# Graph attention on one core: logits of sources added and weights turned on TensorE, one exponential a batch, one more tile by columns

## The chip, the core and the metric

The kernel runs on one core of a Trainium2 chip. The core has engines that run side by side and wait for each other through semaphores: TensorE (PE in the profile; its weight loads are PEld), VectorE (DVE), ScalarE (ACT), GpSimd (POOL) and SyncE (SP). The metric is the device time of one execution in microseconds, lower is better; the time of a kernel is the median of several runs.

## The reference

A graph of 12,500 nodes has 412,500 edges, sorted by their target. Each node has 128 features in four heads of 32, each edge 64.

```python
h = jnp.maximum(_layernorm(x, axis=-1), 0.0)
h = (h @ W_node.T).reshape(num_nodes, H, HD)            # H = 4, HD = 32
e = (edge_features @ W_edge.T).reshape(num_edges, H, HD)
att = jnp.sum(jnp.concatenate([h[src], h[tgt], e], -1) * a, axis=-1)
att = jnp.where(att > 0, att, 0.2 * att)
m = jnp.maximum(segment_max(att, tgt), 0.0)
ex = jnp.exp(att - m[tgt])
denom = segment_sum(ex, tgt) + (num_edges - deg)[:, None] * jnp.exp(-m)
out = x + segment_sum((ex / denom[tgt])[:, :, None] * h[src], tgt)
```

An edge's logit is a sum of three parts: one of its source, one of its target, one of the edge itself. The weights of a target's edges are normed over the edges of that target, and the sources' rows are added up with these weights.

## The kernel before, in words

**Ahead of the loop** the kernel makes a table in device memory with a row of 144 numbers for each node: for each head the 32 projected features, two columns of ones and the two parts of the logit. The normed node features, turned (feature by node), also stay in SBUF as `features`.

**Batches.** The edges are cut into 461 chunks of 896 edges (7 tiles of 128), and 7 chunks make a batch, so 66 batches of 49 tiles. The loop over batches is written out. The order of the instructions on each engine is the order of the calls in that loop (lines 1328 to 1407); no scheduler moves them, and the engines meet only where one waits for a semaphore.

**Rows.** A tile of a batch needs the table rows of its 128 sources in the row buffer `hs`. There are three row buffers, so the rows of batch b + 3 can be brought when the scatter of batch b is done. Rows come in three ways. Most tiles are gathered by POOL (`gather`, one indirect DMA for a tile, line 334); ahead of them stands a memset of one column (`gate`, line 819) that waits for that scatter. One tile of a batch (three quarters of it in even batches) is brought row by row by SP, 32 single-row DMAs at a time (`row_by_row`, line 864), in turn with the loads of the edge features `eft` (line 760). The rest is made anew: ACT (line 885) and DVE (line 883) copy the sources' columns out of `features` one by one into `turned`, at addresses that they read into registers in groups of 32 (TENSOR_LOAD, line 852), and PE multiplies `turned` with the projection `wall` (`put_back`, line 904), whose result ACT copies into `hs` (line 905). `TURNED` says how many tiles come this way: 4 in odd batches, 3 and a quarter in even ones.

**Who copies columns when.** `OF_SCALAR` gives the groups of 32 copies that ACT does in an even and an odd batch, `OF_VECTOR` those of DVE. ACT's stand in `of_scalar` calls between its other work, and what is left is done at the end of the batch (line 1392), so ahead of the next batch's exponential. DVE's stand at named places, of which the first so many in `BEHIND` are taken.

**One batch** runs so. `begin` has PE multiply the edge features (lines 935 and 938), two batches ahead; `choose` has PE add the targets' logits (line 795), one batch ahead. `weigh` and `weigh_part` (lines 962 to 1026) make the weights: DVE copies the sources' logits out of `hs`, turns them (a transpose of blocks of 32), adds them to the product in four parts, applies the leak, finds each target's maximum by two scans (forward and back) and subtracts it (line 1014); ACT takes the exponential in four parts (line 1016); DVE forms the maxima at each target's end in four parts (line 1018) and turns both (line 1021). `mark` makes the one-hot matrix `hot` of the targets (line 958). `collect` has ACT copy the sums of the batch before out of PSUM (line 1120). `scatter` has DVE multiply the rows with the weights, two tiles and then five (line 1089), and PE add them up through `hot` (line 1095), after `collect` has emptied the same PSUM columns. Every second batch `merge` adds two batches' sums to what their targets have so far.

Of the kernel before, what the change touches and what calls it, by code (L numbers as in the profile page):

```python
# [9 lines left out]
F32 = mybir.dt.float32  # L10
# [4 lines left out]
OP = mybir.AluOpType  # L15
# [62 lines left out]
TURNED = 4  # L78
OF_SCALAR = (10, 9)
OF_VECTOR = (5, 5)  # L80
BEHIND = ("rows", "first", "near", "hot", "down", "up")
# [78 lines left out]
def kernel(  # L160
# [567 lines left out]
    both_ps = bank[:, :2 * T * R].rearrange("p (w t r) -> p w t r", w=2, t=T)  # L728
    ex_ps = both_ps[:, 0, :, :]
# [253 lines left out]
    def open_weights(s):  # L983

        s.zst = work.tile([P, T, R], F32, name="zst")
        a = work.tile([P, BUF], F32, name="a")
        s.att, s.m = a[:R, :CE], a[R:2 * R, :CE]
        s.up = ps.tile([P, BANKS * 512], F32, name="up")[:R, :CE]
        s.both = work.tile([P, 2, T, R], F32, name="both")

    def weigh_part(s, t0, t1):

        zst, att, up, m, both = s.zst, s.att, s.up, s.m, s.both
# [3 lines left out]
        def grouped(what, g):  # L997
            return what.rearrange("r (t g i) -> r g t i", g=NQT, i=R)[:, g, t0:t1, :]
# [8 lines left out]
        nc.vector.tensor_scalar(att[:, e0:e1], up[:, e0:e1], 0.2, None, op0=OP.mult)  # L1007
        on_half(s, nc.vector.tensor_tensor(z, up[:, e0:e1], att[:, e0:e1], op=OP.max))  # L1008
# [6 lines left out]
        for g in range(NQT):  # L1015
            nc.scalar.activation(both[g * R:(g + 1) * R, 0, t0:t1, :], grouped(att, g), AF.Exp)  # L1016
        for g in range(NQT):
            nc.vector.scalar_tensor_tensor(both[g * R:(g + 1) * R, 1, t0:t1, :], grouped(s.pen[:, 1:], g), -1.0 / BIG,  # L1018
                                           grouped(up, g), op0=OP.mult, op1=OP.mult)
        if t1 - t0 == T:  # L1020
            nc.vector.transpose(both_ps.rearrange("p w t r -> p (w t r)"), both.rearrange("p w t r -> p (w t r)"))  # L1021
        else:
            for w in range(2):
                nc.vector.transpose(both_ps[:, w, t0:t1, :].rearrange("p t r -> p (t r)"),  # L1024
                                    both[:, w, t0:t1, :].rearrange("p t r -> p (t r)"))
        nc.vector.tensor_copy(own, both_ps[:, 1, t0:t1, :s.chunks * H].rearrange("p t (q h) -> p t q h", h=H))
# [56 lines left out]
    def scatter(s):  # L1083
# [3 lines left out]
        for t0, t1 in ((0, FIRST), (FIRST, T)):  # L1087
# [3 lines left out]
            of_vector("rows" if t1 == T else "first")  # L1091
# [215 lines left out]
    with tc.manual_schedule():  # L1307
# [20 lines left out]
        for b in range(NBT - 1):  # L1328
# [30 lines left out]
            if b < NBT - 2:  # L1359
                mark(s)  # L1360
# [29 lines left out]
            if b == NBT - 3:  # L1390
                mark(batch(b + 1))
            of_scalar(spare[ENG.Activation])
# [309 lines left out]
```

## Time and profile before

| | |
|---|---|
| time, median of 3 runs | 6768.51 us (6765.73 to 6787.56) |
| the profiled execution: its own time, its span | 6719.83 us, 6718.1 us |
| busy, share of the span: PE, DVE, ACT, POOL | 27%, 40%, 38%, 42% |
| copies of single columns: ACT (L885), DVE (L883) | 18624 of 187 ns, 9888 of 142 ns |
| gathers by POOL (L334, from the table) | 2887 of 947 ns |
| row-by-row DMAs by SP (L864) | 7072 |
| scatter on PE (L1095) | 1820 of 680 ns |

The busy time is an average over stages that differ, and no engine is busy for half of the span. What matters in a kernel like this is the chain of waits from batch to batch: who waits for whom at the points where buffers are handed over. A row of the timeline gives the start, the time from the first start to the last end, the engine, the line, the operation, the tile written and read with its shape, the count, and in brackets how long the engine was idle before and what ended that. "issue" means that the profile shows nothing that the engine waited for.

### The profile page before, as it was taken

What the parts mean: (1) busy time and instruction counts of PE and PEld (TensorE: products, weight loads), DVE (VectorE), ACT (ScalarE), POOL (GpSimd) and SP (SyncE); (2) the same over time, 40 slices, a digit from 0 to 9 for tenths busy, and PEclk for the clock granted to TensorE, in tenths of its full rate; (3) what the DMA queues carried; (4) which work ended last, traced back from release to release, by engine and by line L of the source; (5) the groups of instructions that cost most, each with busy time, mean ns of one, the idle gap of its engine ahead of it and who ended that gap; (6) DMA issues with size and microseconds to landing.
All of it is one profiled execution on the core that took longest, in us unless ns stands there. A gap on an engine that the chain in (4) does not pass through costs nothing. (4 is left out here: it accounts for less than half of the span.)

```text
span 6718.1 us, 65140 instructions
## 1 busy us (share of the span) xinstructions
PE 1803.4 (27%) x4569; PEld 724.3 (11%) x4569; DVE 2718.8 (40%) x13514; ACT 2583.9 (38%) x20492; POOL 2797.8 (42%) x3018
## 2 busy tenths in 40 slices
PE   4223123223123232222232232133123223312323
PEld 3101001011011011010011011011011001101111
DVE  4434334344344243353343344344334334434445
ACT  4134334334344344344344344344334434433420
POOL 4453443343443443533533443443453353344351
PEclk8566566566566566665666566566566566656666
DMA  4322222222222222222222222222222222222221
GB/s 115 94 61 58 61 61 64 61 61 62 57 63 65 59 64 60 64 65 57 64 66 61 65 66 61 62 63 61 67 64 65 59 61 67 62 66 65 64 66 43
DMA packets 225620, 432.22 MB, mean 64 GB/s; under 512 B 92316, under 2 KB 125094, under 8 KB 225144
## 3 DMA queue, kind: packets, MB, share of 16 engines
q0 software_dynamic: 94240, 216.84, 13.5%
q1 hardware_dynamic: 100664, 145.09, 7.4%
q10 hardware_dynamic: 30240, 66.08, 2.8%
q14 instruction: 438, 3.59, 0.2%
q8 instruction: 38, 0.62, 0.0%
HBM read 412.21 MB, written 15.53 MB: 64 GB/s over the span
## 5 line engine op out<-in xcount | busy, mean ns | idle before, releaser
L885 ACT COPY turned<-features 128x1 f32 x18624 | 2053.1, 187 | 3473.0 <-issue 3469.9
L334 POOL DMA_INDIRECT hs<-table,ends x2887 | 2734.6, 947 | 1006.8 <-issue 895.0
L819 POOL MEMSET gate<- 128x1 f32 x63 | 6.2, 99 | 2758.7 <-PE pa L1095 2751.6
L1095 PE MATMUL pa<-hs,hot 128*128 128x504 f32 x1820 | 937.0, 680 | 531.5 <-ACT r L1120 478.6
L904 PE MATMUL more<-wall,turned 128*128 128x144 f32 x430 | 155.5, 457 | 3011.5 <-ACT hs L905 2985.0
L883 DVE COPY turned<-features 128x1 f32 x9888 | 681.8, 142 | 691.9 <-issue 689.8
L1021 DVE STREAM_TRANSPOSE exr<-both 128x448 f32<-128x448 f32 x65 | 42.9, 660 | 1530.4 <-ACT both L1016 1529.8
L1095 PEld LDWEIGHTS pa<-hs,hot 128*128 128x128 f32 x1820 | 398.5, 223 | 1045.4 <-issue 505.2
L1089 DVE TENSOR_TENSOR hs<-hs,exr 128x1848 f32<-128x1848 f32 (+1 forms) x130 | 456.6, 3515 | 0.0
L904 PEld LDWEIGHTS more<-wall,turned 128*128 128x128 f32 x430 | 91.5, 265 | 3093.8 <-ACT hs L905 3027.1
L938 PE MATMUL z<-eft,wa 128*32 128x512 f32 (+1 forms) x792 | 354.4, 592 | 61.5 <-DMA eft<-in_ef 61.4
L935 PE MATMUL z<-eft,wa 128*64 128x512 f32 (+1 forms) x132 | 85.6, 738 | 960.1 <-DMA eft<-in_ef 814.5
L1014 DVE TENSOR_TENSOR a<-z,a 32x896 f32<-32x896 f32 (+1 forms) x67 | 71.7, 1070 | 643.5 <-issue 643.3
L1120 ACT COPY r<-pa 32x70 f32<-32x70 f32 (+1 forms) x1040 | 263.6, 253 | 119.3 <-PE pa L1095 88.2
L1004 DVE TENSOR_TENSOR up<-z,zst 32x224 f32<-32x224 f32 (+2 forms) x268 | 104.3, 389 | 429.8 <-PE z L795 418.9
L795 PE MATMUL z<-near_dst,near_rows 128*32 128x512 f32 (+1 forms) x528 | 214.7, 550 | 30.5 <-DVE run L1154 22.6
L1018 DVE SCALAR_TENSOR_TENSOR both<-pen_sb,up 32x224 f32<-32x224 f32 (+2 forms) x268 | 100.3, 374 | 202.2 <-issue 201.7
L1016 ACT ACTIVATE both<-a 32x224 f32<-32x224 f32 (+2 forms) x268 | 102.8, 384 | 172.1 <-DVE a L1014 126.1
L789 DVE TENSOR_TENSOR near_dst<-near_dst,least 128x1792 f32<-128x1792 int32 x66 | 132.4, 2006 | 20.3 <-DMA near_dst<-in_dstc 20.3
L958 DVE TENSOR_TENSOR hot<-exr,key 128x1568 f32<-128x1568 f32 x65 | 116.4, 1791 | 59.3 <-PE pa L1095 57.1
L1009 DVE TENSOR_TENSOR_SCAN up<-pen_sb,z 32x896 f32<-32x896 f32 (+1 forms) x67 | 133.6, 1994 | 2.3
L1194 DVE TENSOR_TENSOR acc<-acc,up 128x70 f32 x461 | 105.1, 228 | 70.7 <-issue 48.6
(203 smaller groups left out, 1503.4 us busy)
## 6 DMA issues: line engine op xcount, KB each, us to landing
hs<-table SPq DMA_DIRECT2D x7072, 0.6 KB
eft<-in_ef SPq DMA_DIRECT2D x231, 448.0 KB
near_dst<-in_dstc ACTq DMA_DIRECT2D x128, 448.0 KB
hs<-table,ends POOLq DMA_INDIRECT x2887
near_rows<-near SPq DMA_DIRECT2D x461, 0.5 KB
pen_sb<-pens SPq DMA_DIRECT2D x66, 98.1 KB
xg<-in_xh SPq DMA_DIRECT2D x13, 448.0 KB
out<-xg SPq DMA_DIRECT2D x13, 448.0 KB
```

Source lines behind the costliest of these rows:

```text
L334: load = nc.gpsimd.indirect_dma_start(out=rows, out_offset=None, in_=of[:, :], in_offset=bass.IndirectOffsetOnAxis(ap=at, axis=0), engine_ ...
L789: nc.vector.tensor_tensor(hot, s.near_dst.bitcast(I32), least[:, s.b, :, None].to_broadcast([P, 2, CE]), op=OP.is_equal)
L795: s.made = own_half(s, nc.tensor.matmul(s.z[:, part], near_rows[:, s.b % 2, k, :], hot[:, k, part], start=False, stop=(k == 1), skip_group ...
L883: nc.vector.tensor_copy(s.turned[:, i:i + 1], column)
L885: nc.scalar.copy(s.turned[:, i:i + 1], column)
L904: nc.tensor.matmul(back_ps, s.turned[:, i * P:(i + 1) * P], wall, start=True, stop=True)
L938: s.made = own_half(s, nc.tensor.matmul(s.z[:, part], wa3[:, j + s.b % 2 * (SB + 1), :], s.eft[:, j, part], start=False, stop=(j == NEXT - ...
L958: nc.vector.tensor_tensor(s.hot.rearrange("p t q r -> p (t q) r"), rows_ps[:, None, :].to_broadcast([P, T * CB, W]), key[:, :, None].to_br ...
L1009: on_half(s, nc.vector.tensor_tensor_scan(up[:, e0:e1], s.pen[:, e0:e1], z, 0.0, op0=OP.add, op1=OP.max))
L1089: nc.vector.tensor_tensor(rows, rows, ex_ps[:, t0:t1, :CB * H, None].to_broadcast([P, t1 - t0, CB * H, HB]), op=OP.mult)
L1095: scattered[s.b] = nc.tensor.matmul(wide_ps[:, g, :], s.hot[:, t, g * NEXT:g * NEXT + SB, :].rearrange("p q r -> p (q r)"), flat[:, at:at ...
L1120: nc.scalar.copy(r[h * W:(h + 1) * W, q:q + NEXT * len(of) - NEXT + 1:NEXT, :], block)
```

## The change

`TURNED` becomes 5: odd batches make five tiles by columns, even ones four and a quarter, and POOL gathers one tile less in each batch (45 and 44 become 44 and 43). `OF_SCALAR` becomes (10, 10) and `OF_VECTOR` (9, 8): in an even and in an odd batch ACT does 10 and 10 groups of copies, not 10 and 9, and DVE 9 and 8, not 5 and 5. `BEHIND` has new places on DVE: "middle" (between the products of the scatter), "own" (after the sources' logits are copied), "up" (after the first scan), and, in even batches, "leaky" (ahead of it); "end" is named but not reached.

The sources' logits are no longer turned and added by DVE: PE multiplies them with the identity and adds the result to the product in PSUM (new line 998). ACT takes one exponential over 32 partitions and 896 columns (new line 1011), DVE forms the maxima in one step (1012), into the lower half of the same tile `both`, and PE turns both together in seven transposes (1015). `mark` moves into `weigh_part`, behind these transposes in the program's text. The products of the scatter are made for two, two and three tiles.

```diff
-TURNED = 4
-OF_SCALAR = (10, 9)
-OF_VECTOR = (5, 5)
-BEHIND = ("rows", "first", "near", "hot", "down", "up")
+TURNED = 5
+OF_SCALAR = (10, 10)
+OF_VECTOR = (9, 8)
+BEHIND = ("rows", "first", "near", "middle", "hot", "own", "down", "up", "leaky", "end")
...
-    both_ps = bank[:, :2 * T * R].rearrange("p (w t r) -> p w t r", w=2, t=T)
-    ex_ps = both_ps[:, 0, :, :]
+    both_ps = bank[:, :2 * T * R].rearrange("p (t w r) -> p t w r", w=2, t=T)
+    ex_ps = both_ps[:, :, 0, :]
...
-        s.both = work.tile([P, 2, T, R], F32, name="both")
+        s.both = work.tile([2 * R, CE], F32, name="both")
...
-        nc.vector.transpose(zst[:, t0:t1, :].rearrange("p t i -> p (t i)"),
-                            logits[:, t0:t1, :].rearrange("p t i -> p (t i)"))
-        for g in range(NQT):
-            on_half(s, nc.vector.tensor_tensor(grouped(up, g), grouped(s.z, g),
-                                               zst[g * R:(g + 1) * R, t0:t1, :], op=OP.add))
+        for t in range(t0, t1):
+            s.made = own_half(s, nc.tensor.matmul(s.z[:, t * P:(t + 1) * P], logits[:, t, :], ident,
+                                                  start=False, stop=True, skip_group_check=True))
+        of_vector("own")
         z = s.z[:, e0:e1]
-        nc.vector.tensor_scalar(att[:, e0:e1], up[:, e0:e1], 0.2, None, op0=OP.mult)
-        on_half(s, nc.vector.tensor_tensor(z, up[:, e0:e1], att[:, e0:e1], op=OP.max))
+        on_half(s, nc.vector.tensor_scalar(att[:, e0:e1], z, 0.2, None, op0=OP.mult))
+        on_half(s, nc.vector.tensor_tensor(z, z, att[:, e0:e1], op=OP.max))
+        of_vector("leaky")
...
-        for g in range(NQT):
-            nc.scalar.activation(both[g * R:(g + 1) * R, 0, t0:t1, :], grouped(att, g), AF.Exp)
-        for g in range(NQT):
-            nc.vector.scalar_tensor_tensor(both[g * R:(g + 1) * R, 1, t0:t1, :], grouped(s.pen[:, 1:], g), -1.0 / BIG,
-                                           grouped(up, g), op0=OP.mult, op1=OP.mult)
-        if t1 - t0 == T:
-            nc.vector.transpose(both_ps.rearrange("p w t r -> p (w t r)"), both.rearrange("p w t r -> p (w t r)"))
...
+        nc.scalar.activation(both[:R, e0:e1], att[:, e0:e1], AF.Exp)
+        nc.vector.scalar_tensor_tensor(both[R:, e0:e1], s.pen[:, e0 + 1:e1 + 1], -1.0 / BIG, up[:, e0:e1],
+                                       op0=OP.mult, op1=OP.mult)
+        for t in range(t0, t1):
+            nc.tensor.transpose(both_ps[:, t, :, :].rearrange("p w r -> p (w r)"), both[:, t * P:(t + 1) * P],
+                                ident[:2 * R, :2 * R])
+        if s.b < NBT - 2:
+            mark(s)
...
-        for t0, t1 in ((0, FIRST), (FIRST, T)):
+        for t0, t1 in ((0, FIRST), (FIRST, 2 * FIRST), (2 * FIRST, T)):
...
-            of_vector("rows" if t1 == T else "first")
+            of_vector("rows" if t1 == T else "middle" if t0 else "first")
...
-            if b < NBT - 2:
-                mark(s)
...
                 put_back(later, 3)
+                put_back(later, 4)
...
+            of_vector("end")
```

How the change stands on the engines is shown for an even batch. On PE, from the edge product of a later batch (L938) to the next addition of targets (L795), before:

```order
L938 MATMUL z<-eft,wa_84 32x384 x3
L904 MATMUL more<-wall,turned 128x144 x3
L909 MATMUL more<-wall,turned 32x144
L1095 MATMUL pa<-hs,hot 128x504 x14
L795 MATMUL z<-near_dst,near_rows 32x512 x2
```

and now:

```order
L938 MATMUL z<-eft,wa_84 32x384 x3
L998 MATMUL z<-ident,logits 32x128 x7
L1015 MATMUL exr<-ident,both 128x64 x7
L904 MATMUL more<-wall,turned 128x144 x4
L909 MATMUL more<-wall,turned 32x144
L1088 MATMUL pa<-hs,hot 128x504 x14
L795 MATMUL z<-near_dst,near_rows 32x512 x2
```

The addition of the sources' logits (L998) now stands behind the edge product, and the first product of the columns (L904) behind the transposes of the weights (L1015).

On ACT, from the last copies ahead of the exponential, before:

```order
L885 COPY turned<-features 128x1 x32
L1016 ACTIVATE both<-a 32x224 x4
L905 COPY hs<-more 128x144
L780 DMA near_dst<-in_dstc 128x1x896 x2
L905 COPY hs<-more 128x144
L852 TENSOR_LOAD numbers
L885 COPY turned<-features 128x1 x32
L905 COPY hs<-more 128x144
L1120 COPY r<-pa 32x35 x2
```

and now:

```order
L885 COPY turned<-features 128x1 x32
L1011 ACTIVATE both<-a 32x896
L905 COPY hs<-more 128x144
L780 DMA near_dst<-in_dstc 128x1x896 x2
L905 COPY hs<-more 128x144
L852 TENSOR_LOAD numbers
L885 COPY turned<-features 128x1 x32
L905 COPY hs<-more 128x144 x2
L1113 COPY r<-pa 32x35 x2
```

One exponential stands for four, and one more put-back copy stands ahead of the emptying of the sums. Ahead of the first row shown ACT now has eight groups of copies since the end of the odd batch before, and had seven.

On DVE, from the sources' logits to the exponent and the maxima, before:

```order
L1000 COPY logits<-hs 128x7x28
L1001 STREAM_TRANSPOSE zst<-logits 128x224
L1004 TENSOR_TENSOR up<-z,zst 32x7x32 x4
L1007 TENSOR_SCALAR a<-up 32x896
L1008 TENSOR_TENSOR z<-up,a 32x896
L1009 SCALAR_TENSOR_TENSOR up<-pen_sb,z 32x896
L1012 SCALAR_TENSOR_TENSOR a<-pen_sb,up 32x896
L852 TENSOR_LOAD numbers
L883 COPY turned<-features 128x1 x32
L1014 TENSOR_TENSOR a<-z,a 32x896
L1018 SCALAR_TENSOR_TENSOR both<-pen_sb,up 32x224 x4
```

and now (in an odd batch without the group between L1003 and L1005):

```order
L996 COPY logits<-hs 128x7x28
L852 TENSOR_LOAD numbers
L883 COPY turned<-features 128x1 x32
L1002 TENSOR_SCALAR a<-z 32x896
L1003 TENSOR_TENSOR z<-z,a 32x896
L852 TENSOR_LOAD numbers
L883 COPY turned<-features 128x1 x32
L1005 SCALAR_TENSOR_TENSOR up<-pen_sb,z 32x896
L852 TENSOR_LOAD numbers
L883 COPY turned<-features 128x1 x32
L1008 SCALAR_TENSOR_TENSOR a<-pen_sb,up 32x896
L852 TENSOR_LOAD numbers
```

Four groups of copies stand where one stood; the fourth follows the last row shown, ahead of the subtraction.

More of the change, by code (lines that the diff above doesn't have):

```diff
@@ L983, in open_weights @@
     def open_weights(s):
-        s.zst = work.tile([P, T, R], F32, name="zst")
         a = work.tile([P, BUF], F32, name="a")
@@ L988, in open_weights @@
         s.up = ps.tile([P, BANKS * 512], F32, name="up")[:R, :CE]
[L989 removed]
+        s.both = work.tile([2 * R, CE], F32, name="both")
     def weigh_part(s, t0, t1):
[L993 removed]
+        att, up, m, both = s.att, s.up, s.m, s.both
         own = s.hs.rearrange("p (t q) (h k) -> p t q h k", t=T, h=H)[:, t0:t1, :s.chunks, :, AW - 1]
         e0, e1 = t0 * P, t1 * P
[L997 to L998 removed]
         nc.vector.tensor_copy(logits[:, t0:t1, :s.chunks * H].rearrange("p t (q h) -> p t q h", h=H), own)
[L1001 to L1005 removed]
+        for t in range(t0, t1):
+            s.made = own_half(s, nc.tensor.matmul(s.z[:, t * P:(t + 1) * P], logits[:, t, :], ident,
+                                                  start=False, stop=True, skip_group_check=True))
+        of_vector("own")
         z = s.z[:, e0:e1]
[L1007 to L1008 removed]
+        on_half(s, nc.vector.tensor_scalar(att[:, e0:e1], z, 0.2, None, op0=OP.mult))
+        on_half(s, nc.vector.tensor_tensor(z, z, att[:, e0:e1], op=OP.max))
+        of_vector("leaky")
         on_half(s, nc.vector.tensor_tensor_scan(up[:, e0:e1], s.pen[:, e0:e1], z, 0.0, op0=OP.add, op1=OP.max))
@@ L1014, in weigh_part @@
         on_half(s, nc.vector.tensor_tensor(att[:, e0:e1], z, mp, op=OP.subtract))
-        for g in range(NQT):
-            nc.scalar.activation(both[g * R:(g + 1) * R, 0, t0:t1, :], grouped(att, g), AF.Exp)
-        for g in range(NQT):
-            nc.vector.scalar_tensor_tensor(both[g * R:(g + 1) * R, 1, t0:t1, :], grouped(s.pen[:, 1:], g), -1.0 / BIG,
-                                           grouped(up, g), op0=OP.mult, op1=OP.mult)
-        if t1 - t0 == T:
[L1021 to L1026, printed above, removed]
+        nc.scalar.activation(both[:R, e0:e1], att[:, e0:e1], AF.Exp)
[6 more added lines that the diff above has]
+            mark(s)
+        nc.vector.tensor_copy(own, both_ps[:, t0:t1, 1, :s.chunks * H].rearrange("p t (q h) -> p t q h", h=H))
     spans = ((0, EARLY), (EARLY, T))
```

## The prediction

> **What bounds the kernel now.** I read the waits first, then the gates of the gathers, then one batch engine by engine. The waits (who waited <- for whom: us in total, times, longest):
>
> ```profile
> POOL gate L819 <- PE pa L1095: 2751.6, 62, 61.9
> DVE exr L1021 <- ACT both L1016: 1529.8, 60, 31.9
> PE pa L1095 <- ACT r L1120: 478.6, 61, 12.9
> ```
>
> Read as a ring: POOL may gather the rows of a batch only when PE has scattered the batch three before it (the ring of three row buffers). PE waits in every batch for ACT to empty the sums (L1120). DVE waits 25 us in every batch for ACT's exponential. ACT stands at both places, and POOL, the engine that the share of busy time puts first, stands idle 41% of the span. The gates (the small memset L819 ahead of each batch's gathers), from 2990 us to the end and from 540 to 2690 us:
>
> ```profile
> L819 POOL MEMSET gate<- x35: 98/99/100, 2996.7 to 6365.0; 128x1 f32 x35
> L819 POOL MEMSET gate<- x22: 98/99/100, 542.1 to 2688.6; 128x1 f32 x22
> ```
>
> So two batches (an odd and an even one) last 2 x 3368.3/34 = 198.1 us late in the run and 2 x 2146.5/21 = 204.4 us early. Batch 28, an even one of the later kind, in the order of time, first POOL, then ACT, then PE:
>
> ```profile
> 3099.54 0.10 POOL L819 MEMSET gate<- 128x1 f32 x1 [47.32 <-PE pa L1095]
> 3100.40 0.94 POOL L334 DMA_INDIRECT hs<-table,ends  x1 [0.76 <-issue]
> ...
> 3155.33 0.94 POOL L334 DMA_INDIRECT hs<-table,ends  x1 [0.30 <-issue]
> 3197.03 0.10 POOL L819 MEMSET gate<- 128x1 f32 x1 [40.75 <-PE pa L1095]
> ```
> ```profile
> 3102.60 2.41 ACT L885 COPY turned<-features 128x1 f32 x25 [0.95 <-issue]
> ...
> 3160.12 0.19 ACT L885 COPY turned<-features 128x1 f32 x1 [1.21 <-issue]
> ...
> 3163.61 1.67 ACT L885 COPY turned<-features 128x1 f32 x17 [0.51 <-issue]
> 3165.19 0.56 ACT L885 COPY turned<-features 128x1 f32 x5
> 3165.66 0.78 ACT L1016 ACTIVATE both<-a 32x224 f32<-32x224 f32 x2
> 3166.45 0.79 ACT L1016 ACTIVATE both<-a 32x224 f32<-32x224 f32 x2
> 3167.26 0.28 ACT L905 COPY hs<-more 128x144 f32<-128x144 f32 x1
> 3168.47 0.28 ACT L905 COPY hs<-more 128x144 f32<-128x144 f32 x1 [0.94 <-PE more L904]
> 3179.66 2.13 ACT L1120 COPY r<-pa 32x70 f32<-32x70 f32 x8
> 3186.84 3.06 ACT L885 COPY turned<-features 128x1 f32 x32 [0.94 <-issue]
> ```
> ```profile
> 3181.84 15.06 PE L1095 MATMUL pa<-hs,hot 128*128 128x504 f32 x28 [7.18 <-ACT r L1120]
> ```
>
> Two speeds are seen. While POOL's gathers run, ACT gives out one copy in 1.40 us (0.19 busy, 1.21 "issue"); some 6 to 8 us after the last gather the copies come at 0.1 us again (17 in 1.67). I call this the slow stage. It ends about 63 us after the gate. Then ACT works off the 22 copies still ahead of the exponential, does it (gate + 66.1), goes on without a pause worth naming until L1120 is done, PE scatters (16.2 us after the exponential's start), and the next gate opens: 66.1 + 16.2 + 15.2 = 97.5 us. The odd batch takes the rest of the pair, 100.6. DVE in the same even batch:
>
> ```profile
> 3104.26 1.08 DVE L1007 TENSOR_SCALAR a<-up 32x896 f32<-32x896 f32 x1
> 3108.55 2.01 DVE L1012 TENSOR_TENSOR_SCAN a<-pen_sb,up 32x896 f32<-32x896 f32 x1
> 3110.75 1.43 DVE L883 COPY turned<-features 128x1 f32 x22 [0.20 <-issue]
> 3124.42 0.15 DVE L883 COPY turned<-features 128x1 f32 x1 [1.25 <-issue]
> 3134.92 1.08 DVE L1014 TENSOR_TENSOR a<-z,a 32x896 f32<-32x896 f32 x1 [10.35 <-issue]
> 3167.27 0.66 DVE L1021 STREAM_TRANSPOSE exr<-both 128x448 f32<-128x448 f32 x1 [26.37 <-ACT both L1016]
> 3171.09 2.03 DVE L883 COPY turned<-features 128x1 f32 x32 [0.41 <-issue]
> 3176.97 4.96 DVE L1089 TENSOR_TENSOR hs<-hs,exr 128x4620 f32<-128x4620 f32 x1
> ```
>
> DVE has some 22 copies at hand when the slow stage reaches it, then it too goes at 1.40 us. It has subtracted (L1014) at gate + 36, is done four small steps later and then idles for 26 us. What DVE is spared there is worth nothing; what ACT gets more is paid.
>
> **The change, part by part.** (1) One tile less is gathered in each batch. 45 gathers start in 3100.40 to 3155.33, so one in 1.25 us; the slow stage ends that much sooner: **-1.25 us a batch**. Below nothing is excluded, and more than one spacing would need gathers that slow each other, which the even spacing denies.
>
> (2) Four more groups of 32 copies in a batch on average: 3.5 on DVE, half a one on ACT. ACT's goes into the odd batch, at its end, so it stands ahead of the next even batch's exponential (54 copies instead of 22 after the slow stage). One group costs 3.06 + 0.94 (the row at 3186.84): **+4.0 us in the even batch**.
>
> (3) DVE's groups. "own" is issued while DVE waits for PE. "leaky", "up" and "down" stand in the slow stage, where DVE idled, but 96 copies at 1.40 us are 134 us, more than the stage has. By its end DVE should be inside "up" (even batch: adding done at gate + 8, 22 to 27 copies of "leaky" at hand, the rest at 1.40 us, a pause like the 10.35 us ahead of L1014, the first scan near gate + 30, some 20 copies of "up" by gate + 61). What is left then goes fast: about 1 us of "up", a scan of 2.0, "down" 2.4, L1014's subtraction 1.1, so the exponent is ready near gate + 68. ACT reaches it at 66.1 - 1.25 + 4.0 = gate + 68.9. **Nothing is charged**, the cover is about 1 us; if DVE is late it costs what it is late by (a rival). Behind the exponential DVE's last product moves out by the group "middle" (2.03 + 0.41) and by the later marking, some 3.5 us; PE's start moves by 3.3 (below), and PE works 8 us on the first four tiles before it needs that product.
>
> (4) One exponential of 896 columns instead of four of 224. From the two shapes in the trace,
>
> ```profile
> L1016 ACT ACTIVATE both<-a 32x224 f32<-32x224 f32 x260 | 100.5, 386 | 159.9 <-DVE a L1014 114.1 <-issue 43.6
> L1016 ACT ACTIVATE both<-a 32x128 f32<-32x128 f32 x4 | 1.2, 308 | 0.1
> L516 PE MATMUL pt<-ident,hn 128*128 128x128 f32 x156 | 32.7, 320 | 6.4 <-DVE hn L510 3.0 <-ACT hn L507 1.7 <-issue 1.0
> ```
>
> (386 - 308)/96 = 0.81 ns a column, so 386 + 672 x 0.81 = 0.93 us against 1.57 (3165.66 to 3167.24): **-0.65 us**.
>
> (5) The weights are turned by PE. The seven transposes stand on PE between the exponential and the first product of the columns (L904), whose result ACT copies out right after the exponential. Today that product is done early in the slow stage,
>
> ```profile
> 3105.72 0.51 PE L904 MATMUL more<-wall,turned 128*128 128x144 f32 x2
> ```
>
> and ACT goes on in 0.02 us (3167.26). Now ACT waits for seven transposes and a product. A transpose is at most 0.32 us (L516, twice as wide) and at least a third of that: 0.75 to 2.2 us for seven; product and hand-over are the 0.94 of the row at 3168.47. Taken near the upper end, since L516 is the same kind of work: **+2.7 us a batch** (1.7 to 3.2). DVE's own transpose goes, but its marking (L958) now waits for PE's transposes, so nothing returns there.
>
> (6) One more tile to put back: 0.94 + 0.28 on ACT: **+1.2 us a batch**.
>
> (7) PE's adding of the logits stands behind the edge product of the next batch. Later in the run this product is done some 6 us after the gate, in DVE's slack: nothing. Early it waits for a late load:
>
> ```profile
> 1631.61 1.97 PE L935 MATMUL z<-eft,wa 128*64 128x512 f32 x2 [65.85 <-DMA eft<-in_ef]
> 1637.60 2.12 PE L938 MATMUL z<-eft,wa 128*32 128x384 f32 x6
> 1632.31 1.58 ACT L1016 ACTIVATE both<-a 32x224 f32<-32x224 f32 x4
> ```
>
> There the exponential would come at 1631.61 + 8.1 (the product) + 2 (seven small matmuls) + 6.3 (L1007 to L1012) + two groups of 2.4 + 1.1 = 1654, 22 us later. The load is late because SP's last block of 32 rows falls into the slow stage:
>
> ```profile
> 1555.56 10.83 SPq L864 DMA_DIRECT2D hs<-table  x32
> ...
> 1568.55 58.31 SPq L864 DMA_DIRECT2D hs<-table  x32
> ```
>
> SP runs on while the gate comes 22 us later; that is more than the 10.83 us of a block outside the slow stage, so the lag should be gone after one such pair: **+22 us once**.
>
> **Sum.** Odd batch -1.25 - 0.65 + 2.7 + 1.2 = +2.0; even +6.0; a pair +8.0, so 206.1 us. Late part: 17 pairs x 8.0 = +136. Early part: the lag gone, 206.1 - 204.4 = 1.7 on 10.5 pairs = +18. Once +22. In all +176 on the profiled execution (6719.8): 6896. The median shown (6768.5) is 48.7 above the profiled one; I leave that difference as it is: **6945 us**.
>
> **A rule that speaks against the change.** Right where DVE copies, at 3110.75, POOL goes on in its step:
>
> ```profile
> 3110.38 0.95 POOL L334 DMA_INDIRECT hs<-table,ends  x1 [0.30 <-issue]
> 3111.63 0.94 POOL L334 DMA_INDIRECT hs<-table,ends  x1 [0.30 <-issue]
> ```
>
> The Trainium skill ("SBUF — State Buffer", section "SBUF: two separate sides") says that a float32 copy of DVE from SBUF to SBUF holds the port through which GpSimd writes descriptors, so that gathers wait. By that rule 3.5 x 32 more copies would lengthen the gathers, and so the slow stage. The rows show the step unchanged at 1.25 us with DVE copying and without it, so this trace does not bear it out for copies of one column.
>
> **Rivals.** *DVE or PE becomes the late one* (13%): PE's small matmuls fall to the slow pace, or DVE's pause ahead of a scan lies behind the slow stage. For: PE does nothing in the slow stage (stretch, its length, then busy us and instructions of PE, PEld, DVE, ACT, POOL, PE's clock),
>
> ```profile
> 3112.00:3160.00 48.00, 0.00 (x0) 0.00 (x0) 4.30 (x18) 6.70 (x35) 33.60 (x36) 0.50 0.24 57
> ```
>
> so its pace there is unknown, and DVE's cover is 1 us. Price up to 4.5 us a batch: 35 batches x 4.5 + 21 x 4.5 more, 6945 + 250 = 7195, with half of it 7070. *The lag of SP stays* (7%): each early odd batch pays the 22 us: 10 x 20 = 7145. *The gathers and SP set the pace, not ACT* (11%): a pair follows the slow stage, ACT's additions hide in it, and the lag ends: 30 pairs x -2.5 = -75, 6695. For it: SP runs through the early part almost without rest. Against: PE's wait for L1120 in 61 batches. It decides if ACT no longer ends last at the scatter. *Gains and costs meet* (5%): transposes at their lower bound, the early lag gone without the 22: about 6768. *Copies that block POOL* (2%): 112 x 0.15 us a batch, 61 batches, about 7970.
>
> **How the numbers follow.** The forecast, slower by ACT's added work, has 62%; its own range is 6860 to 7030 (transposes and DVE's cover at their bounds). Slower in all 62 + 13 + 7 + 2 = 84%, the same 5%, faster 11%. Within 0.3% is taken as no change: the three runs of before lie that far apart. The range 6775 to 7130 leaves out the faster case, the blocked gathers and the upper part of the late DVE or PE, about 2 in 10.
>
> **What would show it.** Right: 43 or 44 gathers and 69 us from gate to exponential in the even batches; ACT idle 2 to 3 us ahead of the first L905 after the exponential, named as waiting for PE; PE still waiting for ACT's emptying of the sums; late pairs near 206 us. Wrong: DVE named as what the exponential waits for, long and often; the small matmuls 1 us and more apart in the slow stage; pairs below 198 us.

## The result, and the profile after

The changed kernel takes 6998.4 us (median; 6987.6 to 7004.0) against 6767.1 us of the kernel before on the same chip: ratio 1.033, 95% interval 1.031 to 1.036. That is 231 us more; 177 were forecast. The traced execution of the change spans 6994.9 us, that of before 6718.1. The traced run of before lies 47 us under its median and that of the change 2 us under its own, so the two traces differ by 277 us; 46 of these come from which executions were traced.

The waits of the changed kernel (who waited <- for whom: us in total, times, longest):

```profile
POOL gate L819 <- PE pa L1088: 3125.2, 63, 75.0
PE exr L1015 <- DVE both L1012: 2274.3, 39, 66.8
DVE a L1002 <- remote: 1984.9, 53, 54.9
PE exr L1015 <- ACT both L1011: 1473.8, 27, 62.3
PE pa L1088 <- ACT r L1113: 476.4, 62, 8.2
ACT both L1011 <- DVE a L1010: 270.4, 40, 87.3
ACT hs L905 <- PE more L904: 228.1, 168, 2.1
```

The ring is the same: POOL waits for the scatter (L1088, formerly L1095), the scatter for ACT's emptying of the sums (L1113, formerly L1120). What is new: DVE waits some 37 us in nearly every batch ahead of its first step on the logits (L1002), ACT waits for DVE's subtraction (L1010) ahead of 40 of the 67 exponentials, and for PE behind it. Most of the 270.4 us for L1010 lies at the kernel's start and end and in one batch near 2950 us (11.8); in the even batches of the loop it is 0.6 to 3.3 us each, some 40 us in all. The gates, late and early in the run:

```profile
L819 POOL MEMSET gate<- x35: 98/98/100, 2987.2 to 6534.5; 128x1 f32 x35
...
L819 POOL MEMSET gate<- x23: 98/98/100, 465.8 to 2766.4; 128x1 f32 x23
```

A late pair of batches lasts 2 x 3547.3/34 = 208.7 us (198.1 before), an early one 2 x 2300.6/22 = 209.1 (204.4 before). An even batch (42) in the order of time: POOL, then ACT, then PE.

```profile
4660.69 0.10 POOL L819 MEMSET gate<- 128x1 f32 x1 [48.86 <-PE pa L1088]
4661.56 0.94 POOL L334 DMA_INDIRECT hs<-table,ends  x1 [0.77 <-issue]
...
4715.24 0.94 POOL L334 DMA_INDIRECT hs<-table,ends  x1 [0.30 <-issue]
4763.67 0.10 POOL L819 MEMSET gate<- 128x1 f32 x1 [47.50 <-PE pa L1088]
```
```profile
4720.86 0.19 ACT L885 COPY turned<-features 128x1 f32 x1 [1.21 <-issue]
...
4723.69 1.49 ACT L885 COPY turned<-features 128x1 f32 x15 [0.51 <-issue]
4726.12 3.28 ACT L885 COPY turned<-features 128x1 f32 x32 [0.94 <-issue]
4730.37 0.95 ACT L1011 ACTIVATE both<-a 32x896 f32<-32x896 f32 x1 [0.97 <-DVE a L1010]
4733.33 0.28 ACT L905 COPY hs<-more 128x144 f32<-128x144 f32 x1 [2.00 <-PE more L904]
...
4735.08 0.28 ACT L905 COPY hs<-more 128x144 f32<-128x144 f32 x1 [1.47 <-DMA near_dst<-in_dstc]
4737.63 3.06 ACT L885 COPY turned<-features 128x1 f32 x32 [2.28 <-issue]
```
```profile
4749.98 13.57 PE L1088 MATMUL pa<-hs,hot 128*128 128x504 f32 x28 [7.15 <-ACT r L1113]
```

44 gathers, as forecast, end 1.3 us sooner. The slow stage is there as before. Behind it ACT now has a whole group more, waits 0.97 us for DVE, does one exponential of 0.95 us, and waits 2.00 us for PE ahead of the first put-back. PE's last small matmuls of this batch and of the odd one after it (its gate is the second one above), then DVE in both:

```profile
4666.49 0.71 PE L998 MATMUL z<-ident,logits 128*32 128x128 f32 x5
...
4772.77 0.71 PE L998 MATMUL z<-ident,logits 128*32 128x128 f32 x5
```
```profile
4689.28 1.08 DVE L1002 TENSOR_SCALAR a<-z 32x896 f32<-32x896 f32 x1 [35.34 <-issue]
...
4718.07 2.02 DVE L1005 TENSOR_TENSOR_SCAN up<-pen_sb,z 32x896 f32<-32x896 f32 x1 [10.43 <-issue]
...
4727.13 2.03 DVE L883 COPY turned<-features 128x1 f32 x32
4729.19 1.08 DVE L1010 TENSOR_TENSOR a<-z,a 32x896 f32<-32x896 f32 x1
...
4818.84 1.09 DVE L1002 TENSOR_SCALAR a<-z 32x896 f32<-32x896 f32 x1 [34.93 <-remote]
```

PE's small matmuls are over at gate + 6.5, yet DVE starts on their sum at gate + 28.6; in the odd batch they are over at gate + 9.8, and DVE starts at gate + 55. So DVE's chain, which was over at gate + 36 before, now ends at gate + 70. The means over the 17 late pairs of each trace, in us:

| from the gate | even before | even after | odd before | odd after |
|---|---|---|---|---|
| last gather's end | 56.8 | 55.5 | 55.7 | 54.4 |
| DVE's subtraction ends | 36.2 | 70.0 | 42.6 | 67.6 |
| ACT's last copy ends | 65.9 | 68.8 | 69.9 | 69.6 |
| exponential starts | 65.8 | 70.1 | 69.8 | 69.6 |
| exponential to scatter | 16.2 | 19.6 | 17.4 | 20.7 |
| scatter to next gate | 14.5 | 14.5 | 14.4 | 14.2 |

### The profile page after: what moved, and what is told of

Its sections match the earlier page's. It is cut to its first block, busy times and chain, and to the rows that moved or that the text cites. A ratio compares the mean times of both kernels' runs of the same rounds, so it can differ in the third digit from the quotient of the medians.

```text
span 6994.9 us, 75615 instructions
## 1 busy us (share of the span) xinstructions
PE 1919.4 (27%) x6079; PEld 896.2 (13%) x6079; DVE 2970.4 (42%) x19950; ACT 2648.9 (38%) x21313; POOL 2737.3 (39%) x2956
## 5 line engine op out<-in xcount | busy, mean ns | idle before, releaser
L885 ACT COPY turned<-features 128x1 f32 x19584 | 2138.8, 187 | 3491.7 <-issue 3486.9
L334 POOL DMA_INDIRECT hs<-table,ends x2825 | 2674.0, 947 | 985.2 <-issue 880.5
L883 DVE COPY turned<-features 128x1 f32 x16864 | 1138.6, 143 | 946.2 <-issue 939.8
L1015 PE MATMUL exr<-ident,both 64*128 64x64 f32 x462 | 65.5, 316 | 3806.5 <-DVE both L1012 2274.3
L1088 PE MATMUL pa<-hs,hot 128*128 128x504 f32 x1820 | 925.2, 673 | 490.3 <-ACT r L1113 476.4
L1002 DVE TENSOR_SCALAR a<-z 32x896 f32<-32x896 f32 (+1 forms) x67 | 71.7, 1070 | 2313.6 <-remote 1984.9
L1015 PEld LDWEIGHTS exr<-ident,both 64*128 64x128 f32 x462 | 54.2, 215 | 3824.0 <-ACT both L1011 3824.0
L1088 PEld LDWEIGHTS pa<-hs,hot 128*128 128x128 f32 x1820 | 394.4, 221 | 995.0 <-ACT r L1113 502.7
L904 PE MATMUL more<-wall,turned 128*128 128x144 f32 x554 | 234.5, 527 | 392.4 <-ACT hs L905 372.4
L938 PE MATMUL z<-eft,wa 128*32 128x512 f32 (+1 forms) x792 | 320.0, 547 | 1.1 <-DMA eft<-in_ef 0.9
L1113 ACT COPY r<-pa 32x70 f32<-32x70 f32 (+1 forms) x1040 | 263.2, 253 | 53.7 <-PE pa L1088 38.9
L795 PE MATMUL z<-near_dst,near_rows 128*32 128x512 f32 (+1 forms) x528 | 215.2, 551 | 13.1 <-DVE near_dst L789 13.1
L1005 DVE TENSOR_TENSOR_SCAN up<-pen_sb,z 32x896 f32<-32x896 f32 (+1 forms) x67 | 133.6, 1994 | 172.3 <-issue 132.3
L904 PEld LDWEIGHTS more<-wall,turned 128*128 128x128 f32 x554 | 138.8, 311 | 474.0 <-ACT hs L905 445.6
L905 ACT COPY hs<-more 128x144 f32<-128x144 f32 x277 | 76.4, 276 | 320.6 <-PE more L904 228.1
L1011 ACT ACTIVATE both<-a 32x896 f32<-32x896 f32 (+1 forms) x67 | 62.7, 935 | 270.4 <-DVE a L1010 270.4
L998 PE MATMUL z<-ident,logits 128*32 128x128 f32 x924 | 118.8, 282 | 73.8 <-DVE logits L996 69.0
L1008 DVE TENSOR_TENSOR_SCAN a<-pen_sb,up 32x896 f32<-32x896 f32 (+1 forms) x67 | 132.7, 1981 | 2.1
```

The source lines that it names most:

```text
L334: load = nc.gpsimd.indirect_dma_start(out=rows, out_offset=None, in_=of[:, :], in_offset=bass.IndirectOffsetOnAxis(ap=at, axis=0), engine_ ...
L795: s.made = own_half(s, nc.tensor.matmul(s.z[:, part], near_rows[:, s.b % 2, k, :], hot[:, k, part], start=False, stop=(k == 1), skip_group ...
L883: nc.vector.tensor_copy(s.turned[:, i:i + 1], column)
L885: nc.scalar.copy(s.turned[:, i:i + 1], column)
L904: nc.tensor.matmul(back_ps, s.turned[:, i * P:(i + 1) * P], wall, start=True, stop=True)
L938: s.made = own_half(s, nc.tensor.matmul(s.z[:, part], wa3[:, j + s.b % 2 * (SB + 1), :], s.eft[:, j, part], start=False, stop=(j == NEXT - ...
```

## The experiments

Theory W: the loss is ACT's added work, paid because ACT stands last at the exponential and at the scatter. Rival L: DVE (or PE ahead of it) has become late. Rival G: the gathers set the pace. Some expectations name further rivals.

One thing has to be known to read the numbers. The runs were made on several chips, each set beside the kernel before on the same chip. On the chips of the first comparison and of the runs with filler the kernel before takes 6767 and 6765 us; on the three others 4006, 4001 and 3999 us. The record does not tell the chip from the set of runs, so what is called a chip with or without the slow stage below could also be a matter of the set. What goes with the difference in every trace is the slow stage. Two stretches within gathers (its length, then busy us and instructions of PE, PEld, DVE, ACT, POOL, then PE's clock, DMA share, GB/s), the changed kernel on the first chip:

```profile
4672.00:4714.00 42.00, 0.00 (x0) 0.00 (x0) 5.15 (x34) 6.02 (x32) 31.63 (x35) 0.50 0.25 59
```

and the same kernel on a chip of the second kind:

```profile
2050.00:2090.00 40.00, 20.70 (x49) 9.50 (x50) 34.45 (x231) 24.20 (x208) 30.01 (x30) 0.64 0.43 119
```

POOL gathers at the same step on both (the median distance of two gathers is 1.25 us). On the first, DVE and ACT get out 34 and 32 instructions meanwhile, on the second 231 and 208.

**The change again, on a chip without the slow stage.** No edit.

> The changed kernel itself, not edited, beside the kernel before on the chip of these runs. If what is met is what the first two traces show (one instruction in 1.40 us on ACT, DVE and SP while the gathers run, the kernel before at 6767 us), the change takes 6998 us again, ratio 1.033. If what is met is what the first four experiments show (no such slow stage, the kernel before at 4006 us), theory P (the gathers set the time, the fifth tile saves 1.25 us a batch, 62 x 1.25 = 78 us, and PE's turning gives it back): within 20 us of the kernel that differs from it by one group only, 4022 us, so 4000 to 4040 us, ratio 1.000 to 1.008. Rival Q (the group that was moved to DVE there costs what was lost): 3943 us, ratio 0.984.

3920.4 us against 4000.6: ratio 0.980 (0.978 to 0.982). Neither number was met, rival Q's is the nearer. So the same change is 3.3% slower with the slow stage and 2.0% faster without it. Without it POOL hardly ever waits; its row for the gate:

```profile
POOL gate L819 <- PE pa L1088: 56.9, 2, 45.6
```

and its gates, of the change and then of the kernel before with two groups moved (below; as fast as the kernel before within 0.2%):

```profile
L819 POOL MEMSET gate<- x63: 98/117/124, 245.1 to 3821.2; 128x1 f32 x63
```
```profile
L819 POOL MEMSET gate<- x63: 98/113/124, 241.8 to 3917.7; 128x1 f32 x63
```

57.7 us a batch against 59.3: 1.6 less, the one gather (1.25) and 0.35 more. Rival G is how the kernel works there. (The record has no trace of the unedited kernel before from such a chip; this one stands in for it.)

**ACT made to stand last, in both kernels.** 80 copies on ACT at the end of 61 batches; the filler's values go nowhere. They do for ACT's place in the ring what the slow stage did, and more.

```diff
+FILL, FILLS = 384, 80
...
             of_scalar(spare[ENG.Activation])
+            for _ in range(FILLS if 1 <= b <= BOTH else 0):
+                nc.scalar.copy(filler, filler)
```

> The kernel before with 80 copies of 128x384 added on ACT at the end of each of 60 batches (the filler's values go nowhere): an estimated 0.47 us each, 38 us a batch, so that ACT stands last at the exponential, as it did in the first trace, while no slow stage is needed for it. On a chip where the kernel before takes some 4000 us this is to be the base for the next three runs: ACT's own series (19 groups of 4.0 us, two fillers of 38, exponentials, put-backs, sums and merging, about 26 us) makes a pair of about 178 us, 5500 us in all.

> The changed kernel with the same filler on ACT. Theory W (the loss of the first comparison is ACT's added work, paid wherever ACT stands last): a pair is longer than that of the filled kernel before by 4.0 us (one more group) + 2 x (1.2 put-back + 2.0 waiting for PE - 0.65 exponential) = 9.1 us, 30 pairs, 273 us more than the kernel before with filler. Rival S (the loss comes from the slow stage itself, by DVE's and PE's lateness in it, and not from ACT's added work): without a slow stage it gains, as without filler: 80 us less than the kernel before with filler.

This set met a chip with the slow stage (before: 6765 us), so the filler's 49 us a batch came on top of it. With filler the kernel before takes 9758.8 us and the changed one 10104.3: 345 us more, where W expected 273 and rival S 80 less. The gates (62 steps) of the first and the second:

```profile
L822 POOL MEMSET gate<- x63: 98/98/100, 357.3 to 9611.1; 128x1 f32 x63
```
```profile
L822 POOL MEMSET gate<- x63: 99/99/101, 371.9 to 9940.5; 128x1 f32 x63
```

9253.8/31 = 298.5 and 9568.6/31 = 308.7 us a pair: +10.2, against 9.1 expected. DVE's subtraction ends at gate + 77 there and the exponential starts at gate + 120 or later, so DVE's lateness has no part in it. The filled change has five waits of ACT for that subtraction, and none of them lies between the first gate and the last:

```profile
ACT both L1014 <- DVE a L1013: 177.9, 5, 96.2
```

In means, exponential to scatter takes 3.2 us more in both batches; gate to exponential 5.2 more in the even and 1.4 less in the odd. The even batch's 5.2 is not fully accounted for: one group costs 5.0 (next experiment) and the gathers should take off 1.25, so 1.4 are left over. Rival S falls. That the sign turns only by ACT's place was meant to be shown without a slow stage, and the chip did not allow it; what is shown is that with ACT last and DVE far from last the loss is there, and not smaller.

**One group of ACT's to DVE.** With filler first:

```diff
-OF_SCALAR = (10, 10)
-OF_VECTOR = (9, 8)
+OF_SCALAR = (10, 9)
+OF_VECTOR = (9, 9)
```

> The changed kernel with the filler and one group of copies fewer on ACT in the odd batches (on DVE instead). Without filler this was 100 us slower than the change. Theory W: with ACT last it is 4.0 us a pair faster than the filled changed kernel, 30 x 4.0 = 120 us. Rival S: slower than the filled changed kernel, or the same.

9954.7 us, 149.7 less than the filled change: W, with the price nearer 5 than 4. The gates give 9420.6/31 = 303.9 us a pair, 4.8 less than the filled change's 308.7:

```profile
L822 POOL MEMSET gate<- x63: 98/98/100, 367.6 to 9788.2; 128x1 f32 x63
```

The even exponential moves from gate + 120.4 to 115.4. Without filler:

> The changed kernel with one group of copies fewer on ACT in each odd batch (10 and 9) and one more on DVE there (at the place behind the leaky step). Theory W (ACT's work ahead of the exponential sets the time): the even batch's exponential comes 4.0 us sooner, some 30 pairs x 4.0 = 120 us, so about 6878 us. Rival L (DVE ends last at the even batch's exponential, where its subtraction ends at gate + 70.0 and ACT's last copy at gate + 68.8): nothing is won in the even batch, since DVE still ends at gate + 70, and the odd batch's subtraction (now gate + 67.6, ACT at 69.6) moves out by a group of up to 5 us: 7000 to 7090 us. Rival G (gathers and SP set the pace): within 20 us of 6998.

> The changed kernel with one group of copies fewer on ACT in each odd batch, one more on DVE (behind the leaky step), without filler, once more, for a chip with the slow stage (the kernel before at 6767 us, the change at 6998 us). Theory W alone (DVE's cover is enough): 150 us less than the change, as the same step was worth with the filler: 6848 us. Rival L (without filler DVE ends last at the even exponential, its subtraction at gate + 70.0 against ACT's 68.8): the even batch wins nothing, the odd one loses up to 3 us: 6990 to 7090 us. Where the slow stage is not met (before at 4000 us), 4022 us again.

Both met chips without the slow stage, where those numbers do not apply: 4021.8 us (ratio to before 1.005) and 4024.7 (1.006), so some 100 us slower than the change itself by the ratios, and as expected for the second. There ACT is not last. POOL now has to wait for the scatter:

```profile
POOL gate L819 <- PE pa L1088: 116.4, 22, 44.5
```

That is of the first of the two: 22 waits where the change had 2. The reading is that the group lengthens DVE's way to the scatter. One and the same edit is worth -150 us where ACT stands last and +100 where the gathers set the pace and DVE has no slack. What it would give on the first chip without filler, where DVE already ends 1.2 us behind ACT, stays open.

**The weights turned by DVE again,** four exponentials, one transpose of DVE, the product waiting for nothing of PE:

```diff
-        nc.scalar.activation(both[:R, e0:e1], att[:, e0:e1], AF.Exp)
...
-        for t in range(t0, t1):
-            nc.tensor.transpose(both_ps[:, t, :, :].rearrange("p w r -> p (w r)"), both[:, t * P:(t + 1) * P],
-                                ident[:2 * R, :2 * R])
+        for g in range(NQT):
+            nc.scalar.activation(both[g * R:(g + 1) * R, 0, t0:t1, :], grouped(att, g), AF.Exp)
...
+            nc.vector.transpose(both_ps.rearrange("p w t r -> p (w t r)"), both.rearrange("p w t r -> p (w t r)"))
```

> The changed kernel with the filler and the weights turned by DVE again (four exponentials, no wait of ACT for PE). Theory W: per batch ACT pays 0.65 us more for the exponentials and 2.0 us less for waiting, 60 x 1.35 = 81 us less than the filled changed kernel. Rival C (ACT's wait for PE is covered, DVE's products set the scatter): within 20 us of the filled changed kernel.

10058.9 us, 45.4 less than the filled change; W expected 81. Exponential to scatter is 2.0 us shorter in both batches, more than the 1.35 of W's sum: the exponentials take 0.64 us more and the wait for PE 1.85 less, and the second put-back and the gap behind it are 0.47 and 0.34 shorter. So the wait counts in full there (rival C falls). But 2.0 us over 61 batches are 122 us, not 45. The rest comes back at another place, ACT's exponentials of the merging, which wait for DVE; first the change with filler, then this kernel:

```profile
ACT up L1163 <- DVE up L1161: 116.0, 35, 5.9
```
```profile
ACT up L1171 <- DVE up L1169: 201.4, 35, 6.8
```

85 us: DVE, given its transpose back, comes later to them. So turning by PE, with the one exponential that goes with it, costs 2.0 us a batch on ACT's way and gives 1.4 of them back on average. Without filler:

> The changed kernel with the weights turned by DVE again (four exponentials of 224 columns, one transpose of DVE), all else as in the change. Theory W (ACT's 2 us of waiting for PE behind the exponential is paid in full in every batch): the way from the exponential to the scatter, 19.7 and 20.7 us, shrinks by 2.2 us, 62 batches: about 6862 us. Rival C (that wait is covered: DVE's products, not ACT's emptying of the sums, let PE start): within 25 us of 6998.

Here the chip was one without the slow stage: 3943.1 us, ratio 0.985 (0.981 to 0.989); the change itself is at 0.980 on another such chip. The price of the wait does not show where the gathers set the pace.

**The fifth tile by columns alone,** adding and turning by DVE:

```diff
-TURNED = 4
-OF_SCALAR = (10, 9)
-OF_VECTOR = (5, 5)
+TURNED = 5
+OF_SCALAR = (10, 10)
+OF_VECTOR = (9, 8)
...
+                put_back(later, 4)
```

> The kernel before with the fifth tile by columns alone (10 and 10 groups on ACT, 9 and 8 on DVE at the changed kernel's places, DVE's product in three parts, marking ahead of it); logits are added and weights turned by DVE as before. Theory W: a pair gains 2 x 1.25 us from the gathers and pays 4.0 (ACT's group) + 2 x 1.2 (put-backs), +3.9: 30 pairs, 6767 + 117 = 6884 us, and down to 6830 if SP's lag in the early odd batches ends here too. Rival L (DVE is late because PE's small matmuls are finished late): DVE, which needs no small matmul here, ends ahead of ACT, as theory W has it. Rival L2 (DVE is late because its own copies fill the slow stage): the subtraction ends at gate + 69 to 71 in even batches here too, 20 to 40 us more, 6905 to 6925. Rival G: 6767 or faster.

3939.2 us, ratio 0.984 (0.980 to 0.988), on the same chip without the slow stage. It is most of the change's 2.0%. What it does on the first chip was not measured.

**Adding by DVE, turning by PE.**

```diff
-        for t in range(t0, t1):
-            s.made = own_half(s, nc.tensor.matmul(s.z[:, t * P:(t + 1) * P], logits[:, t, :], ident,
-                                                  start=False, stop=True, skip_group_check=True))
+        nc.vector.transpose(zst[:, t0:t1, :].rearrange("p t i -> p (t i)"), ...)
+        for g in range(NQT):
+            on_half(s, nc.vector.tensor_tensor(grouped(up, g), grouped(s.z, g), ..., op=OP.add))
```

> The changed kernel with the logits added by DVE again (its transpose and four additions), and PE turning the weights as in the change. Where the slow stage is (before at 6767 us): rival L (DVE is late because PE's small matmuls are finished late in the slow stage): the even exponential comes 1.25 us sooner, 31 x 1.25 = 39 us, 6959 us; rival L2 (DVE is late because its own copies fill the slow stage): within 15 us of 6998. Where it isn't (before at 4006 us): if PE's turning alone gives the fifth tile's gain back, as long as the changed kernel, 4000 to 4030 us; if it takes adding and turning by PE together, 3940 to 3955 us, as with either one undone.

4003.5 us, ratio 1.0005 (0.999 to 1.002), without the slow stage. That lies in the range named for "as long as the changed kernel", but the changed kernel itself is faster (3920.4 on the same chip). So turning by PE with DVE still adding takes the whole gain, and with PE adding too it does not (0.980). POOL's row is like that of the moved group:

```profile
POOL gate L819 <- PE pa L1094: 121.0, 31, 45.3
```

These rows fit one reading, which was not tested apart: whatever lengthens the way from the gathers' landing over DVE to the scatter costs there, and PE's adding makes room for PE's turning. For the first chip this run tells nothing.

**Groups into DVE's idle time, in the kernel before** (a place for copies between the maxima, L1018, and the transpose, L1021):

```diff
-OF_SCALAR = (10, 9)
-OF_VECTOR = (5, 5)
-BEHIND = ("rows", "first", "near", "hot", "down", "up")
+OF_SCALAR = (9, 8)
+OF_VECTOR = (6, 6)
+BEHIND = ("rows", "first", "near", "hot", "down", "idle", "up")
...
+        of_vector("idle")
```

> The kernel before, nothing of the change, with one group of copies fewer on ACT in each batch (9 and 8) and one more on DVE (6 and 6), at a new place between the maxima (L1018) and the transpose (L1021), where DVE idled 26 us in the slow stage. Theory W: each group taken off ACT ahead of an exponential is worth up to 4.0 us in the odd batches (62 copies were left there behind the slow stage) and some 3 us in the even ones (22 were left): a pair -7, 30 pairs, 6767 - 210 = 6557 us; less (6620) where DVE's new group ends later than the exponential. Rival G (the slow stage alone sets the gate to exponential): within 20 us of 6767. Rival L3 (DVE's group ends late, behind the slow stage, and holds up the transpose): 6767 or slower.

> The kernel before with one group of copies fewer on ACT in each batch and one more on DVE between the maxima (L1018) and its transpose, without filler, once more, for a chip with the slow stage. Theory W: a pair -7 us, 6767 - 210 = 6557 us; 6620 where DVE's new group ends later than ACT's exponential could start. Rival L3 (that group holds up the transpose by as much as it spares ACT): 6750 us or slower. Where the slow stage is not met (before at 4000 us), 4011 us again.

4011.1 us (ratio 1.002, 1.001 to 1.004) and 4008.0 (1.002, 1.001 to 1.003), both times without the slow stage. There ACT has time to spare (in the first of the two it waits for DVE's subtraction ahead of 67 exponentials, 957 us in all), and DVE no longer idles 26 us ahead of its transpose. Whether it gains 150 to 210 us on the first chip stays open.

## Why the prediction was right, and where it was off

**What bounds the kernel** held: POOL waits for the scatter, the scatter for ACT, and ACT's additions are paid. The filled kernels show that they are paid with DVE out of the way (+10.2 us a pair; the third prices one group, the fourth the wait). Of the signs named for being right, 70.1 us from gate to exponential (69 named), ACT's idle 2.0 us ahead of the first put-back and PE's wait for the emptying came; a late pair is 208.7 where 206 was named. One sign of being wrong came in half: DVE is what the exponential waits for, and often, but not for long.

**(1) Gathers, -1.25.** The last gather ends 1.3 us sooner in both batches. In the even batch the gain went into ACT's sum as said (last copy 65.9 + 4.0 - 1.25 = 68.65; measured 68.8). In the odd batch it failed: the exponential starts at 69.6 where 68.5 was due. With filler it is 1.4 us sooner there, so the term is right where ACT is far behind. On average ACT gives out 48 copies in the first 10 us behind an odd gate where it gave 52; why is not shown.

**(2) ACT's group, +4.0.** Right without filler (the same sum); 4.8 to 5.0 with it.

**(3) DVE, 0 with a cover of about 1 us.** This is the step that failed. "The first scan near gate + 30" came at gate + 49 to 63 in the even batches, and the subtraction ended at 70.0 instead of near 68: ACT, ready at 68.8, starts the exponential 1.3 us later, about 40 us in 31 even batches. The rival's cause was there, in another form than the one named: the small matmuls do not fall to 1 us apart (they run from gate + 4.8 to 6.2 in the even batches), but DVE, which waits for them, comes 20 to 35 us after the last of them in the even batches and 28 to 49 in the odd ones, and the copies of "leaky", meant for that time, then stand behind it. That this costs 1.3 us and not 4.5 goes with DVE's copies behind the second scan, which take 2.03 us for 32 again once the stage has ended (the row at 4727.13), as the cover assumed. PE's pace in the stage, which the forecast called unknown, can be read from one batch, the first behind the first gate (357.32): amid the gathers, its 14 small matmuls start 0.11 us apart from 404.22 to 405.66, while ACT's copies come 1.40 us apart, and DVE starts on their sum only at 420.30. No run took this lateness alone away on a chip with the slow stage; it rests on the trace's wait for L1010.

**(4) to (6), -0.65 + 2.7 + 1.2 = +3.25 behind the exponential.** Measured +3.4 and +3.3, but in other shares, so that the sum is met partly by luck: the exponential saves 0.62 (0.95 against 1.57), the wait for PE is 2.0, not 2.7, and in place of the missing 0.7 stand the second put-back (1.47 for 0.94) and the gap ahead of the next group (2.28 for 1.94). The first goes with ACT's issue of a load (near_dst), which now falls between the put-backs and had run under the last copies and the exponentials.

**(7) The lag of SP.** It is gone, as said. Idle time ahead of the edge product L935 in the early part, of PE and of its weight loads added, so half of it is PE's (us, times; 540 to 2690 us of the trace before, 465 to 2770 of that after):

```profile
  DMA eft<-in_ef: 1200.1, 18
```
```profile
  issue: 16.1, 22
```

The 22 us once come out as a number, but mostly not by the step that was named, one early odd batch whose exponential comes 22 us late: behind the second gate no early step is longer than 106.0 us. Instead the first gate comes 12.9 us later (an edge product ahead of it, which waits for its load, starts at 290.10 instead of 281.49) and the step from it to the second is 8.9 longer. In that step the edge product comes at gate + 40 and the exponential at gate + 74.8, 5.4 later than before. That the sum is 21.8 is luck.

**The sum.** By stretches of the traces, up to the second gate +21.8 (22 forecast), the 22 early steps +56 (18 forecast), the next two steps +9 (none; in one of them the exponential waits 11.8 us for DVE), the 35 late steps +188 (140 by 8.0 a pair), the end +2. A late pair is +10.5 for +8.0: 1.3 by DVE in the even batch, 1.1 by the odd batch's gathers, 0.1 elsewhere. An early pair, 209.1 where 206.1 was due, misses by much the same. Against the medians the forecast is 53 us short; against the traces, from which it was worked out, 101 (277 for 176). That the medians make up for half of this is luck: the trace of before happened to lie 47 us under its median. The gathers as the bound (11%, 6695 us) did not come about on this chip, and is what happens on the other kind of chip. Copies that block POOL did not either: 3.5 groups more on DVE leave the gathers 1.25 us apart (44 from 4661.56 to 4715.24), so the rule of the Trainium skill ("SBUF — State Buffer", section "SBUF: two separate sides") is not borne out for copies of one column here. The page ties it to a two-port mode of DVE; whether a copy of one column takes that mode, no run here shows.

## What to carry to other kernels

Price an edit from the engine that stands last at the places where the ring closes, and ask of each engine that you load more how much of the cover is real in the stage where it would run; a cover of 1 us is none. A step that an engine starts in time can still be reported late, so follow the waiter and not only the worker. And look whether the stage that sets the time goes with the kernel or with the chip and the set of runs in which it was measured: here one change is 3.3% slower or 2.0% faster by that alone.

## What the runs showed of the hardware

The slow stage was met in the first comparison and in the runs with filler, and in none of the runs on the three other chips; chip and set of runs are not told apart. The same program takes 6767 us on one and 4000 on another, with POOL's gathers at the same step of 1.25 us, and with ACT and DVE held to about one instruction in 1.40 us while the gathers run on the one and free on the other (34 and 32 instructions in 42 us, 231 and 208 in 40). SP is slowed too: 32 of its single-row DMAs took 59.76 us in the gathers from 4665.11 on and the next 32, behind them, 10.99. PE is not, where it can be seen: 14 matmuls 0.11 us apart, 47 to 48 us behind a gate. It is not tied to copies of one column: the four maxima of DVE (L1018) in batch 28 of the kernel before start at 3136.32, 3137.72, 3139.12 and 3140.52. The profile does not show what holds the engines; that is open.

In that stage an instruction's end and its report can be far apart. The last of PE's small matmuls in batch 43 starts at 4773.21, and the trace's update of PE's semaphore comes at 4818.81, 45 us later, 0.03 us ahead of DVE's start; of DVE's own copies the last one starts at 4783.75 and its update comes at 4793.58. In 56 of the 67 cases the trace has an update of PE's semaphore some 0.1 us or less ahead of DVE's start; in the others, batch 42 among them, it has none there. On a chip without the slow stage DVE starts 0.3 to 0.5 us behind the start of the last small matmul in most batches, and 2.3 us at most.
